# Fused attention and spectral layer: the first q stack on ACT's queue, a load in four, a table and fills in other places

## The chip, the cores and the metric

The kernel runs on one core of one Trainium2 chip. A core has five engines that run their own instruction lists and meet through semaphores: TensorE (PE, matmuls; PEld are its weight loads), VectorE (DVE), ScalarE (ACT), GpSimd (POOL) and SyncE (SP), which here only issues DMAs. SP, ACT and POOL can each issue DMAs; the transfers run on 16 DMA engines. The metric is the device time of one execution in microseconds (us); lower is better.

## The reference

One layer of a transformer with two branches over the same normalized input `xn`. With x of 2 x 2048 x 256 float32:

```python
xn = _layernorm(x, axis=-1)
x = x + _L0_attn_ref(xn, wq, wk, wv, wo) + _L0_ffn_ref(xn, w_freq_real, w_freq_imag, bias)

# attention: 16 q heads of 16, 4 k/v heads shared by groups of 4, rotary, causal
q = _apply_rope((x @ wq).reshape(Bx, Sx, 16, 16), cos, sin)
k = _apply_rope((x @ wk).reshape(Bx, Sx, 4, 16), cos, sin)
v = (x @ wv).reshape(Bx, Sx, 4, 16)
scores = where(causal, einsum('bshd,bthd->bhst', q, k) / 4, -inf)      # k, v broadcast to 16 heads
out = einsum('bhst,bthd->bshd', softmax(scores), v).reshape(Bx, Sx, 256) @ wo

# "ffn": a product in the frequency domain
y = real(ifft(fft(x) @ (w_freq_real + 1j * w_freq_imag))) + bias
```

The second branch is linear in `xn`, so the kernel forms one 256 x 256 matrix of it once (`mff`) and multiplies by that.

## The kernel before, in words

**Blocks and units.** The 4096 rows are cut into eight blocks n of 512 rows (`blocks`, two batches b by four positions j, b running fastest). A block has four units g, each of four q heads: 32 units. For each block: load x (`load_x`, L166), row statistics (`row_stats`, L233, on DVE), the power -1/2 (`row_power`, L241, on POOL), the shift -mean/std (`row_shift`, L247, on DVE), normalization (`norm`, L398, on DVE for block 0, on POOL for the others), PE transposes (`transpose_x`, L405), three projections with `features` (L419): c = 2 gives k and v, c = 0 and 1 the q of two units each. `other_half` (L438) makes a copy with the rotary halves swapped, for blocks 0 and 1 by a PE product and for the rest by DMA; `rotate` (L514) applies cos and sin from a table that `rotary_table` (L276) makes for each j (DVE expands it, PE turns it); `split` (L531) cuts the float32 result into three bf16 parts h, m and l.

**Stacks.** The score products run in bf16 over stacked parts: for each unit a tile `qst` holds seven 16-row groups of q parts, for each block a tile `kst` the matching seven of k. `stack` (L483) fills them by seven 64 KB DMAs straight from the parts (k of every block, and q of unit 0 of block 0); `stack_runs` (L495) takes all other q through DRAM with four larger ones. All of these are issued by SP, through `later` (L389), in one list per block (`sends`).

**Scores.** For each unit the kernel first makes the scores with rows in partitions, to take the row maxima (`maxima`, tiles `sm`, DVE reduces them at L636), writes the negative maxima as three more rows of the q stack (`spread`, with an ACT copy and an ACT-issued DMA of 12 KB), then makes the scores with keys in partitions (`scores`, tiles `st`), ACT takes the exponential (L745), and PE multiplies with v and a column of ones (`values`, tiles `av`, L780). Sums and values go through DRAM to be divided (`put`, `gather`, `invert`, `widen`, `scale`), and `output` (L895) adds both branches to x.

**Order.** The program order of every engine is written by a planner at build time (from L922): each step carries modelled costs and a list of what it needs (`use`, `send`, `through_bank`), steps wait in `streams`, and a loop picks the next PE step: scores ("B"), maxima ("A"), values ("V"), or filling work ("F" and "M": transposes, projections, spectral products). The planner's modelled clocks only choose the order; on the chip engines wait for real semaphores. Three PSUM banks of the ring "st" serve scores, projections and all fillers. Each SP, ACT or POOL instruction list runs strictly in its order.

**The start.** PE first runs 48 transposes of a unit matrix that nothing uses (L968), as a warm-up. `ones` (L370) fills the constant columns of v and rows of k, on DVE for block 0 and on POOL for the others. After the statistics of block 0, `load_late` (L217) has POOL issue six loads of weights. The spectral matrix is made in six PE pieces (tiles `ps_ff` and `ps_mff`) that serve as filling work before and between the first maxima. In the order before, DVE takes block 0's shift, then expands the table of j = 0, then normalizes block 0; DVE takes block 2's statistics just before the first maxima; POOL normalizes block 1 together with block 2, from 34.78 us on, so that block 1's projections come after the first maxima.

Of the kernel before, what the change touches and what calls it, by code (L numbers as in the profile page):

```python
# [23 lines left out]
def tile_attn_plus_spectral_ffn(  # L24
# [29 lines left out]
    nc = tc.nc  # L54
# [96 lines left out]
    def product(to, lhsT, rhs, start, stop):  # L151


        for q in range(0, P, QD):
            nc.tensor.matmul(  # L155
                to[q : q + QD], lhsT[:, q : q + QD], rhs, start=start, stop=stop
            )


    def block_rows(n):  # L160
        b, j = blocks[n]
        return x[b, j * SB : (j + 1) * SB, :].rearrange("(i p) d -> p i d", p=P)
# [1 line left out]
    xt = {}  # L164

    def load_x(n):  # L166
        send("sp", 512, [slot("xt")], [("xt", "in", n)])
        take_slot("xt")
        xt[n] = work.tile([P, NI, D], F32, tag="xt", bufs=2, name=f"xt{n}")
        nc.sync.dma_start(out=xt[n], in_=block_rows(n))  # L170

    take_slot("qst"), take_slot("qst")
    load_x(0)
# [43 lines left out]
    def load_late():  # L217

        for name, src, tag, bufs in (
            ("wre", w_re, "inv", 2), ("dc", dft[0], "inv", 2),  # L220
            ("wim", w_im, "attT", 2), ("ds", dft[1], "avs", 3),
        ):
            take_slot(tag)
            spec[name] = work.tile([P, NK, D], F32, tag=tag, bufs=bufs, name=name)
            nc.gpsimd.dma_start(out=spec[name], in_=src.rearrange("(c p) n -> p c n", p=P))
            send("pool", 256, (), ["spec"])
        nc.gpsimd.dma_start(out=wo_sb, in_=wo.rearrange("(c p) n -> p c n", p=P))
        nc.gpsimd.dma_start(out=bias_sb, in_=bias.partition_broadcast(P))
# [4 lines left out]
    def row_stats(n, i):  # L233
        if i == 0:
            mv[n] = work.tile([P, NI, 2], F32, tag="mv", bufs=2, name=f"mv{n}")
        st = work.tile([P, 6], F32, tag="bn", bufs=3, name=f"bn{n}_{i}")
        nc.vector.bn_stats(st, xt[n][:, i, :])
        nc.vector.bn_aggr(mv[n][:, i, :], st)
        use("dve", 0.53, [("xt", "in", n)], [("mv", n)])

    def row_power(n):  # L241
        rstd[n] = work.tile([P, NI], F32, tag="rs", bufs=2, name=f"rs{n}")
# [3 lines left out]

    def row_shift(n):  # L247
        shift[n] = work.tile([P, NI], F32, tag="sh", bufs=2, name=f"sh{n}")
        nc.vector.scalar_tensor_tensor(
            shift[n], mv[n][:, :, 0], -1.0, rstd[n], ALU.mult, ALU.mult  # L250
        )
        use("dve", 0.2, [("rs", n)], [("sh", n)])

# [125 lines left out]
    def project(n):  # L379
# [2 lines left out]
        b, j = blocks[n]  # L382
        e, eng = (nc.vector, "dve") if n == 0 else (nc.gpsimd, "pool")
        MULT, SUB, CAST, NORM = (0.72, 0.72, 0.46, 0.33) if n == 0 else (1.23, 1.13, 0.63, 0.53)
        raw, sw, swp, part, ra, at = {}, {}, {}, {}, {}, {}
        sends = []
        streams.append(sends)

        def later(out, in_, kb, needs, gives):  # L389


            def go():
                nc.sync.dma_start(out=out, in_=in_)
                send("sp", kb, needs, gives)

            sends.append((-1, -1, "sp", needs, [], go))

        def norm(i):  # L398
            e.tensor_scalar(
                xt[n][:, i, :], xt[n][:, i, :], rstd[n][:, i : i + 1], shift[n][:, i : i + 1],  # L400
                ALU.mult, ALU.add,
            )
            use(eng, NORM, [("sh", n)], [("xn", n, i)])

# [11 lines left out]
            if c == NK - 1:  # L416
                there["xt", n] = clock["pe"]

        def features(c):  # L419
            ps = bank(f"ps_q{n}_{c}")  # L420
            for k in range(NK):
                product(
                    ps, wp[:, k, c, :], xnT[n][:, k, :], start=(k == 0), stop=(k == NK - 1)
                )
            raw[c] = work.tile([P, SB], F32, tag="raw", bufs=3, name=f"raw{n}_{c}")
            at[c] = take_slot("raw")
            nc.scalar.copy(raw[c], ps)  # L427
            through_bank(
                1.83, ["wp", *(("xnT", n, k) for k in range(NK))], "act", 0.48, [("raw", "in", n, c)],
                [("raw", at[c] - ring["raw"])],  # L430
            )
            if n >= 2:
                other_half(c)
# [49 lines left out]
        def stack(c, a_part, f):  # L483
            src = part[c][f * HP : (f + 1) * HP, "hml".index(a_part), :]
            for a in range(len(QPART)):
                if (KPART if c == NK else QPART)[a] == a_part:
                    to = kst[n] if c == NK else qst[n, 2 * c + f]
                    gives = []
                    if a == len(QPART) - 1 if c == NK else a_part == "l":
                        gives = [("kst", n) if c == NK else ("stk", n, 2 * c + f)]  # L490
                        gives += [("part", at[c, "part"])] * (c == NK)
                    needs = [("part", "in", n, c, a_part)]
                    later(to[a * DH : (a + 1) * DH, :, :], src, 64, needs, gives)

        def stack_runs(c, units):  # L495

# [71 lines left out]
        ]  # L568
        for c in (NK, 0, 1):
            table = [("cs", j, 1)] * (n >= 2)  # L570
            pe.append(("pe", ["wp", *table, *xs], ["st", "raw"] + ["sw"] * (n >= 2), lambda c=c: features(c)))
            if n < 2:
                pe.append(("pe", [("raw", "in", n, c)], ["st", "sw"], lambda c=c: other_half(c)))
            if c == NK:
                pe.append(("pe", [("raw", "in", n, NK), ("ones", n)], ["st"], proj_v))
# [383 lines left out]
    def stream(pieces, since=-1, by=-1):  # L959
        streams.append([(since, by, *p) for p in pieces])  # L960
        return streams[-1]
# [11 lines left out]
        row_stats(0, i)  # L973
    row_power(0)
    load_late()
    row_shift(0)
    order_weights()

    def chain(n, starts, late=0):

        norms, pe, rot = project(n)
        eng = norms[0][0]
        stats = [("dve", [("xt", "in", n)], [], lambda i=i: row_stats(n, i)) for i in range(NI)]
        stats.append(("pool", [("mv", n)], [], lambda: row_power(n)))
        stats.append(("dve", [("rs", n)], [], lambda: row_shift(n)))
        s = starts
        if n > 1:
            stream([("sp", [], ["xt"], lambda: load_x(n))], s["load"], s["load"])
        if n:
            stream([("pool", [], [], lambda: ones(n))], s["ones"], s["stats"])  # L990
            stream(stats, s["stats"], s["stats"] + late + 1)
        out_pe = streams.append([]) or streams[-1]
        for k, p in enumerate(pe):
            at = s["pe"] + (k // 2 if n > 1 else 0)
            out_pe.append((at, at + late + 1, *p))
        out_rot = streams.append([]) or streams[-1]
        for p in norms:
            out_rot.append((s["stats"], s["stats"] + late + 2, *p))
        for c, more in ((K, 0), (Q0, 2), (Q1, 5)):
            at = s["rot"] + (more if n > 1 else 0)  # L1000
            for k, p in enumerate(rot[c]):
                out_rot.append((at, at + late + 2 + k // 2, *p))

    def table(j, since):
        expand, turn = rotary_table(j)
        last = [("cs used", at_block[B - 1, j - 2])] if j >= 2 else []
        stream(
            [("dve", last, ["raw", "raw2"], expand)]
            + [("pe", [("trx", j)], ["st"], lambda a=a: turn(a)) for a in range(2)],
            since, since + 3,  # L1010
        )
# [243 lines left out]
```

## Time and profile before

| what | value |
|---|---|
| median of 3 runs (lowest to highest) | 925.84 us (924.08 to 927.47) |
| profiled execution: own time, span | 926.44 us, 924.70 us |
| PE busy | 904.6 us, 98% |
| DVE busy | 748.0 us, 81% |
| ACT busy | 653.7 us, 71% |
| POOL busy | 370.1 us, 40% |
| mean granted clock of PE | 0.995 of full speed |
| chain that ended last, by engine | PE 89%, DVE 5%, ACT 3%, issue, DMA and POOL 1% each |

The span is the time from the first to the last instruction in the record; the execution's own time is 1.74 us longer. Busy shares are of the span. PE is busy nearly throughout, so an idle microsecond of another engine counts only where PE stands and waits for it; such waits can be read from the list of waits and from PE's timeline, each with the line of the instruction that waited and of the one that released it. "issue" names time in which an engine waited for nothing that the profile shows. The granted clock is the share of full speed at which PE was allowed to run.

### The profile page before, as it was taken

The page shows a single profiled execution, that of the slowest core. Times are in us where ns is not written, and L with a number is a line of the kernel's source. Part 1 is how long each engine was busy: PE and PEld are TensorE (multiplying, and loading weights), DVE is VectorE, ACT ScalarE, POOL GpSimd, SP SyncE. Part 2 cuts the span into 40 slices and gives each one's busy share as a digit, 9 for nine tenths or more (in the row PEclk, how much of TensorE's full clock was granted, in tenths as well). Part 3 has the DMA queues.
Part 4 walks back from the last instruction along what each step waited for, and adds up shares of the span by engine and source line. Part 5 has one row for each costly group of instructions (what it writes and reads, how often), then busy time and mean ns, then how long its engine had stood idle before and what let it go on. Part 6 is the DMA issues. An engine that isn't in the chain of part 4 may idle for free.

```text
span 924.7 us, 38985 instructions
## 1 busy us (share of the span) xinstructions
PE 904.6 (98%) x17324; PEld 500.5 (54%) x17324; DVE 748.0 (81%) x1056; ACT 653.7 (71%) x1375; POOL 370.1 (40%) x556
## 2 busy tenths in 40 slices
PE   7999899999999999999999999999999999999997
PEld 4666565655555555555555555555455554645443
DVE  6878697789789996998995999979789988788601
ACT  3266565587757784888865777857688878588784
POOL 7298666824672424822236520311572021102111
PEclk9999999999999999999999999999999999999999
DMA  5435823341244011440002500010133001100000
GB/s 165 119 90 143 199 92 106 97 132 38 65 121 124 27 38 34 112 129 26 14 27 85 150 28 13 27 60 14 31 109 88 15 3 38 49 14 15 27 1 24
DMA packets 41992, 62.13 MB, mean 67 GB/s; under 512 B 8840, under 2 KB 32120, under 8 KB 41824
## 3 DMA queue, kind: packets, MB, share of 16 engines
q1 hardware_dynamic: 32400, 41.18, 16.5%
q0 software_dynamic: 8128, 17.69, 5.9%
q8 instruction: 135, 2.21, 1.0%
q10 hardware_dynamic: 1296, 0.79, 0.3%
q14 instruction: 33, 0.27, 0.1%
HBM read 32.75 MB, written 18.40 MB: 55 GB/s over the span
## 4 chain that ended last, share of the span: by engine, by line
PE 89%; DVE 5%; ACT 3%; issue 1%; DMA 1%; POOL 1%; ACTq 0%; SPq 0%; DVEq 0%; POOLq 0%
PE av L780 24%; PE st L155 22%; PE sm L155 17%; PE sm L631 7%; PE po L155 6%; PE ps_q L155 4%; DVE mx L636 2%; PE sp L155 2%; PE sm L627 2%; PE st L738 2%; ACT es L745 1%; PE ps_x L411 1%; PE st L734 1%; ACT es L747 1%; PE ps_m L671 0%
## 5 line engine op out<-in xcount | busy, mean ns | idle before, releaser
L636 DVE TENSOR_REDUCE mx<-sm 128x2 f32<-128x1024 f32 (+3 forms) x640 | 648.9, 1057 | 87.4 <-PE sm L631 44.1
L745 ACT ACTIVATE es<-st 128x512 f32<-128x512 f32 (+3 forms) x1194 | 552.4, 543 | 179.2 <-PE st L155 145.6
L155 PE MATMUL st<-qst,kst 115*32 115x512 bf16 (+3 forms) x4264 | 327.2, 354 | 1.1 <-ACT es L745 0.4
L780 PE MATMUL av<-es,va 128*32 128x512 f32 (+3 forms) x2560 | 299.9, 529 | 0.6 <-issue 0.3
L155 PE MATMUL sm<-kst,qst 112*32 112x512 bf16 x3072 | 239.1, 379 | 0.1
L155 PEld LDWEIGHTS <-kst 115*32 115x32 bf16 x4608 | 161.1, 95 | 140.6 <-issue 64.8
L752 POOL TENSOR_SCALAR_AFFINE_SELECT es<-es 128x256 f32<-128x256 f32 x192 | 76.7, 406 | 276.0 <-ACT es L745 234.8
L155 PEld LDWEIGHTS <-qst 112*32 112x32 bf16 x3072 | 96.0, 96 | 93.0 <-issue 64.8
L631 PE MATMUL sm<-kst,qst 112*32 112x32 bf16 (+15 forms) x2048 | 122.3, 281 | 0.3 <-issue 0.3
L627 PE MATMUL sm<-mask,ident_h 128*32 128x128 bf16 (+3 forms) x2048 | 100.2, 201 | 1.8 <-DVE mx L636 1.0
L780 PEld LDWEIGHTS av<-es,va 128*32 128x32 f32 x2560 | 85.1, 109 | 28.6 <-ACT avs L791 2.6
L631 PEld LDWEIGHTS <-qst 112*32 112x32 bf16 x2048 | 66.3, 97 | 34.3 <-issue 20.6
L627 PEld LDWEIGHTS <-ident_h 128*32 128x32 bf16 x2048 | 66.1, 96 | 32.2 <-issue 25.5
L906 DVE TENSOR_TENSOR xr<-po,xr 128x256 f32<-128x256 f32 x36 | 15.2, 424 | 51.5 <-PE po L155 49.5
L803 POOL DMA_DIRECT2D res<-avs x30 | 18.2, 606 | 82.7 <-ACT avs L791 79.9
L155 PE MATMUL ps_q<-xnT,wp 128*32 128x512 f32 x384 | 45.4, 600 | 0.0
L747 ACT ACTIVATE es<-sp 128x1024 f32<-128x1024 f32 (+3 forms) x43 | 36.6, 907 | 7.6 <-PE sp L155 7.4
L427 ACT COPY raw<-ps_q 128x512 f32<-128x512 f32 x24 | 14.1, 585 | 35.0 <-PE ps_q L155 35.0
L518 POOL TENSOR_TENSOR ra<-raw,cs 128x512 f32<-128x512 f32 (+1 forms) x21 | 27.4, 1304 | 24.2 <-ACT raw L427 23.0
L738 PE MATMUL st<-qst,kst 115*32 115x480 bf16 (+15 forms) x512 | 36.8, 284 | 0.1
L155 PE MATMUL po<-wo_sb,attT 128*32 128x256 f32 x512 | 34.4, 379 | 0.7 <-ACT attT L869 0.7
L155 PE MATMUL po<-mff,xnT 128*32 128x256 f32 x512 | 34.4, 380 | 0.0
(108 smaller groups left out, 657.0 us busy)
## 6 DMA issues: line engine op xcount, KB each, us to landing
qst<-run SPq DMA_DIRECT2D x62, 128.0 KB
res<-avs POOLq DMA_DIRECT2D x30, 256.0 KB, 3.0
run<-part SPq DMA_DIRECT2D x31, 192.0 KB
qst<-run SPq DMA_DIRECT2D x31, 192.0 KB
xt<-in_L_attn_x_dram SPq DMA_DIRECT2D x8, 512.0 KB
xr<-in_L_attn_x_dram SPq DMA_DIRECT2D x16, 256.0 KB
out_dram<-xr SPq DMA_DIRECT2D x16, 256.0 KB
sw<-raw SPq DMA_DIRECT2D x60, 64.0 KB
```

Of the source, the lines that this page charges most:

```text
L155: nc.tensor.matmul(to[q : q + QD], lhsT[:, q : q + QD], rhs, start=start, stop=stop)
L518: e.tensor_tensor(ra[c][:r], raw[c][:r], cs[j][:r, 0, :], ALU.mult)
L627: nc.tensor.matmul(to[:, at:wd], ident_h[:, q : q + QD], mask[:, q:], start=True, stop=True, skip_group_check=True,)
L631: nc.tensor.matmul(to[:, : at + QD], rows[:, q : q + QD], keys[:, : at + QD], start=False, stop=True, skip_group_check=True,)
L636: nc.vector.tensor_reduce(t["mx"][:, i, 2 * pr : 2 * pr + 2, k], ps[0][:, :, :wd], AX.X, ALU.max)
L738: nc.tensor.matmul(to[:, at:], keys[:, q : q + QD], rows[:, at:], start=False, stop=True, skip_group_check=True,)
L745: nc.scalar.activation(es[u, t, pr][:, e, lo:], ps[:, lo:], AF.Exp, scale=SCALE)
L747: nc.scalar.activation(es[u, t, pr][:, :, lo:], wide[pr][:, :, lo:], AF.Exp, scale=SCALE)
L752: nc.gpsimd.affine_select(out=es[u, t, pr][:, :, lo : lo + P], in_=es[u, t, pr][:, :, lo : lo + P], pattern=[[0, 2], [1, P]], compare_op=A ...
L780: nc.tensor.matmul(av[u][QD * h : QD * (h + 1), lo:], va[at_block[b, t // NI]][:, t % NI, h, :], es[u, t, h // 2][:, h % 2, lo:], start=(t ...
L803: nc.gpsimd.dma_start(out=res[n, c][f], in_=avs[u])
L906: nc.vector.tensor_tensor(xr[n, r][:, e, :], po, xr[n, r][:, e, :], ALU.add)
```

## The change

It has these parts:

- Block 0's x is loaded by four DMAs of 128 KB in place of one of 512 KB, and each statistics step needs only its own quarter.
- The expansion of the first rotary table (`table_0[0]()`) stands ahead of block 0's shift on DVE.
- The shift becomes mean/std, subtracted by `norm`; for blocks 1 to 7 it moves from DVE to POOL.
- The seven DMAs that stack unit 0 of block 0 are issued by ACT (`line=2`), with a list of their own; block 0's k stack and its q runs get separate SP lists.
- `features` is cut into two PE steps, one for each half of the contraction, between which the planner may place others.
- In the planner, the fills of blocks 1 to 7 and their powers need block 0's last k part (`first_keys`), and block 2's statistics need the finished maxima of unit 0 of block 0 (`rows_0`).

In the built program this gives a new order in the first 60 us: block 1 is normalized right after its power, on POOL; its transposes, its k/v and its first q projection stand before the first maxima on PE, and half of the spectral pieces after them; ACT's list has, after the two copies of block 1's transposes, four stack issues, then the copy of raw, an issue, a copy of a spectral piece, an issue, the copy of sw, an issue. Block 2's statistics stand after the first maxima of unit 0, its normalization in the middle of block 1's rotation on POOL. SP sends six of block 1's seven k stack DMAs before the q stacks of units 2 and 3 of block 0. Later the order on all engines differs in small ways.

```diff
     def load_x(n):
-        send("sp", 512, [slot("xt")], [("xt", "in", n)])
+        at = slot("xt")
         take_slot("xt")
         xt[n] = work.tile([P, NI, D], F32, tag="xt", bufs=2, name=f"xt{n}")
-        nc.sync.dma_start(out=xt[n], in_=block_rows(n))
+        step = NI if n else 1
+        for i in range(0, NI, step):
+            send("sp", 128 * step, [at], [("xt", "in", n, k) for k in range(i, i + step)])
+            nc.sync.dma_start(out=xt[n][:, i : i + step, :], in_=block_rows(n)[:, i : i + step, :])
...
     def row_shift(n):
         shift[n] = work.tile([P, NI], F32, tag="sh", bufs=2, name=f"sh{n}")
-        nc.vector.scalar_tensor_tensor(
-            shift[n], mv[n][:, :, 0], -1.0, rstd[n], ALU.mult, ALU.mult
-        )
-        use("dve", 0.2, [("rs", n)], [("sh", n)])
+        e, eng, us = (nc.vector, "dve", 0.2) if n == 0 else (nc.gpsimd, "pool", 0.25)
+        e.tensor_tensor(shift[n], mv[n][:, :, 0], rstd[n], ALU.mult)
+        use(eng, us, [("rs", n)], [("sh", n)])
...
-        sends = []
-        streams.append(sends)
-
-        def later(out, in_, kb, needs, gives):
-
+        lines = [[], [], []]
+        streams.extend(lines)
+
+        def later(out, in_, kb, needs, gives, line=0):
+
+
+            eng = "act" if line == 2 else "sp"
 
             def go():
-                nc.sync.dma_start(out=out, in_=in_)
-                send("sp", kb, needs, gives)
-
-            sends.append((-1, -1, "sp", needs, [], go))
+                (nc.scalar if line == 2 else nc.sync).dma_start(out=out, in_=in_)
+                send(eng, kb, needs, gives)
+
+            lines[line].append((-1, -1, eng, needs, [], go))
...
-                ALU.mult, ALU.add,
+                ALU.mult, ALU.subtract,
...
-        def features(c):
-            ps = bank(f"ps_q{n}_{c}")
-            for k in range(NK):
-                product(
-                    ps, wp[:, k, c, :], xnT[n][:, k, :], start=(k == 0), stop=(k == NK - 1)
-                )
+        def features(c, k):
+            if k == 0:
+                held[c] = bank(f"ps_q{n}_{c}"), take_slot("st")
+            ps, at_st = held[c]
+            product(ps, wp[:, k, c, :], xnT[n][:, k, :], start=(k == 0), stop=(k == NK - 1))
+            use("pe", 0.9, ["wp", ("xnT", n, k), ("st", at_st - ring["st"])], [("ps", at_st)])
+            if k < NK - 1:
+                return
...
-                    later(to[a * DH : (a + 1) * DH, :, :], src, 64, needs, gives)
+                    later(
+                        to[a * DH : (a + 1) * DH, :, :], src, 64, needs, gives,
+                        2 if c < NK else 1 if n == 0 else 0,
+                    )
...
-            pe.append(("pe", ["wp", *table, *xs], ["st", "raw"] + ["sw"] * (n >= 2), lambda c=c: features(c)))
+            pe.append(("pe", ["wp", *table, xs[0]], ["st", "raw"] + ["sw"] * (n >= 2), lambda c=c: features(c, 0)))
+            pe.append(("pe", [xs[1]], [], lambda c=c: features(c, 1)))
...
     load_late()
+    table_0 = rotary_table(0)
+    table_0[0]()
     row_shift(0)
...
-        stats = [("dve", [("xt", "in", n)], [], lambda i=i: row_stats(n, i)) for i in range(NI)]
-        stats.append(("pool", [("mv", n)], [], lambda: row_power(n)))
-        stats.append(("dve", [("rs", n)], [], lambda: row_shift(n)))
+        first_keys = [("part", "in", 0, NK, "l")]
+        rows_0 = [("np", 0, 0)] * (n == 2)
+        stats = [("dve", [("xt", "in", n, i), *rows_0], [], lambda i=i: row_stats(n, i)) for i in range(NI)]
+        stats.append(("pool", [("mv", n), *first_keys], [], lambda: row_power(n)))
+        stats.append(("pool", [("rs", n)], [], lambda: row_shift(n)))
...
-            stream([("pool", [], [], lambda: ones(n))], s["ones"], s["stats"])
+            stream([("pool", first_keys, [], lambda: ones(n))], s["ones"], s["stats"])
```

More of the change, by code (lines that the diff above doesn't have):

```diff
@@ L238, in row_stats @@
         nc.vector.bn_aggr(mv[n][:, i, :], st)
-        use("dve", 0.53, [("xt", "in", n)], [("mv", n)])
+        use("dve", 0.53, [("xt", "in", n, i)], [("mv", n)])
     def row_power(n):
@@ L384, in project @@
         MULT, SUB, CAST, NORM = (0.72, 0.72, 0.46, 0.33) if n == 0 else (1.23, 1.13, 0.63, 0.53)
-        raw, sw, swp, part, ra, at = {}, {}, {}, {}, {}, {}
-        sends = []
-        streams.append(sends)
-        def later(out, in_, kb, needs, gives):
+        raw, sw, swp, part, ra, at, held = {}, {}, {}, {}, {}, {}, {}
+        lines = [[], [], []]
+        streams.extend(lines)
+        def later(out, in_, kb, needs, gives, line=0):
+            eng = "act" if line == 2 else "sp"
             def go():
-                nc.sync.dma_start(out=out, in_=in_)
-                send("sp", kb, needs, gives)
-            sends.append((-1, -1, "sp", needs, [], go))
+                (nc.scalar if line == 2 else nc.sync).dma_start(out=out, in_=in_)
+                send(eng, kb, needs, gives)
+            lines[line].append((-1, -1, eng, needs, [], go))
         def norm(i):
@@ L427, in features @@
             nc.scalar.copy(raw[c], ps)
-            through_bank(
-                1.83, ["wp", *(("xnT", n, k) for k in range(NK))], "act", 0.48, [("raw", "in", n, c)],
-                [("raw", at[c] - ring["raw"])],
+            use(
+                "act", 0.48, [("ps", at_st), ("raw", at[c] - ring["raw"])],
+                [("st", at_st), ("raw", "in", n, c)],
             )
@@ L1004, in table @@
     def table(j, since):
-        expand, turn = rotary_table(j)
+        expand, turn = rotary_table(j) if j else table_0
         last = [("cs used", at_block[B - 1, j - 2])] if j >= 2 else []
         stream(
-            [("dve", last, ["raw", "raw2"], expand)]
+            [("dve", last, ["raw", "raw2"], expand)] * (j > 0)
             + [("pe", [("trx", j)], ["st"], lambda a=a: turn(a)) for a in range(2)],
```

## The prediction

> **What bounds the kernel now.** I read the page first, then busy time by stretch, then TensorE's (PE's) waits, then the chain and the timelines of the first 55 us.
>
> ```profile
> PE 904.6 (98%) x17324; PEld 500.5 (54%) x17324; DVE 748.0 (81%) x1056; ACT 653.7 (71%) x1375; POOL 370.1 (40%) x556
> PEclk9999999999999999999999999999999999999999
> ```
>
> PE is busy 904.6 of 924.7 us at almost full clock. No edit changes the number of columns that PE multiplies, so only what PE loses can be won: 20.1 us of idling, and time at a lowered clock. Where it lies (us from the start; stretch, its length, then busy time by engine):
>
> ```profile
> 0.00:25.00 25.00, 20.25 (x157) 12.21 (x161) 17.55 (x49) 8.12 (x16) 16.41 (x36) 0.93 0.52 161
> 25.00:50.00 25.00, 24.44 (x527) 15.35 (x523) 19.86 (x42) 7.85 (x17) 9.79 (x14) 1.00 0.38 103
> ...
> 100.00:125.00 25.00, 21.29 (x655) 15.63 (x655) 18.71 (x33) 16.06 (x44) 15.75 (x24) 0.93 0.61 163
> ```
>
> 4.75 us are idle in the first 25 us, where 7.14 us more are 48 warm-up transposes that compute nothing; 3.7 us in 100 to 125. The end (875 to 925) idles 8.0 us, and no edit touches it. In the two early stretches the third last number, the granted clock, is 0.93. PE's waits name the causes:
>
> ```profile
> PE st L734 <- issue: 2.2, 1, 2.2
> PE ps_tr L305 <- DVE trx L293: 1.8, 1, 1.8
> ...
> PE ps_x L411 <- POOL xt L399: 0.2, 1, 0.2
> ```
>
> The second is the start. Its chain (start, length, what):
>
> ```profile
> 0.80 4.43 DMA xt<-in_L_attn_x_dram
> ...
> 7.90 1.06 POOL rs L244
> 8.96 0.02 issue
> 8.98 0.16 DVE sh L249
> 9.14 1.17 DVE trx L293 x6
> 10.31 0.04 issue
> 10.36 1.11 PE ps_tr L305 x8
> 11.47 0.10 issue
> 11.56 2.32 PE ps_x L411 x8
> 13.88 2.54 PE ps_q L155 x16
> ```
>
> Load, row statistics, the power on POOL, shift, then the rotary table on VectorE (DVE), and only then normalization: the table stands in line although it needs nothing of the statistics. The two PE groups at the end are slow, and the clock by single microseconds says why (third last number):
>
> ```profile
> 9.00:10.00 1.00, 0.00 (x0) 0.00 (x0) 1.00 (x6) 0.53 (x2) 1.00 (x2) 1.00 0.00 0
> 12.00:13.00 1.00, 1.00 (x4) 0.65 (x5) 0.97 (x5) 0.13 (x1) 1.00 (x3) 0.50 0.99 340
> ```
>
> **The start, edit by edit.** *Load in four.* The first statistics began at 5.25, when the 512 KB had landed; DVE's fills end at 4.63. Four 128 KB pieces are issued one per 0.44 to 0.48 us (the length of SP's load issues), in the same order of bytes, so the first two should be there by 4.63 and the last by about 5.2, and statistics start 0.6 earlier. By the waits in the built program SP and ACT share eight completion lanes; block 1's load is now the ninth issue and waits for wk, which landed at 4.97. Block 1 needs it after 10.5: free.
>
> *Table before the shift.* Eight reductions, 1.63 in all, move into POOL's power (7.57 to 8.95). Statistics end at 6.9 instead of 7.47, table 8.5, power 8.35, shift 8.7 instead of 9.14, and the four normalizations (1.89) follow at once instead of at 10.61: 1.9 earlier. The table's input must have landed by 6.9; it is queued behind the first load only, at 192 KB beside 512 KB in some 3 us. At worst it lands with the last bytes, 7.6, and 0.7 of the 1.9 goes.
>
> *The clock.* The warm-up ends at 8.55, the table's transposes now start there, and the 1.80 us hole closes. The Trainium skill, "TensorE: Matmul & The Clock Gate" (section "HAM oscillation — how this bites in real kernels"), asks for no idle gap over about 3.4 us; by it this hole cost 1.8 and nothing more. The trace differs: after it the clock is 0.50 from 11.7 to 15.1, and again from 107.3 to 110.7 after a hole of 2.2; two gaps of 0.7 us each (16.4, 20.4) did nothing. The measurement decides: 3.4 us at half speed cost 1.7. Block 0's transposes then take 1.25 instead of 2.32. Walked through: transposes from 9.65 to 11.4 (last normalized piece 10.6), copies to 12.05, first projection done at 13.2 instead of 16.42. **3.2 us early**, of which DVE's parts and PE's third projection (20.5 instead of 23.7) inherit all; by the skill's rule it would be 1.5.
>
> *Block 1's projection as the next filling.* It replaces half of the spectral products as PE's work ahead of the first scores, and needs POOL's normalization of block 1: power done at 8.35, six load issues (4.46), two fills of 2.55, power 1.6, shift 0.3, four normalizations at 0.54 end at 21.95. PE arrives at 20.5 and would take 0.62: **1.0 lost**.
>
> *First q stack by ACT.* SP had all fourteen stack issues in one line:
>
> ```profile
> 20.10 4.50 SPq L393 DMA_DIRECT2D kst<-part  x7
> 24.73 5.03 SPq L393 DMA_DIRECT2D qst<-part  x7
> ```
>
> so the stack landed at 32.0 although its last part was made at 26.6. On ACT the seven have their own line, but ACT runs in order: four issues come after both copies of block 1's transposes (23.4), then copy raw, issue, copy of a spectral product, issue, copy sw, and the last. With 0.65 to 0.72 per issue the last ends near 29.6 and lands 2.2 later (as SP's last, 29.76 to 32.0), at 31.8. PE gets there at 31.9, with 2.2 us more of work behind it; its old waits of 0.33 (31.7) and 0.21 (38.06) go: **0.5 won**. What queues behind ACT's issues is POOL's rotation of block 1, which needs sw (29.0). SP also sends block 1's keys before the q units 2 and 3, which land near 43; units 2 starts after 49: free.
>
> *Block 2 behind the first maxima.* Its normalization now follows most of block 1's rotation on POOL. From 29.0: k 6.53 (as 46.93 to 53.46), q0 7.83, half of q1 3.98, power 1.4, cast 0.7, shift 0.3, subtraction 1.24, normalization 2.15: 53.1. PE, from 31.9 by its own rows, comes to block 2's transposes near 51.5. The wait is 0 if POOL's start is 1.5 earlier and 2.5 if PE meets no other wait; the near row (0.21 for the same wait) pulls down, the sum says 1.3. I take **1.0 lost**.
>
> *The rest.* Shift on POOL for the other blocks: DVE stood 1.04 in it at 228.16, and PE then idled 0.62 for DVE: **0.6 won**. Projections in two pieces: the same eight products, which already waited for each half separately (begun at 13.81, second half copied at 14.5); they only let scores stand between. Fills "behind" block 0's parts keep their place on POOL, after the loads, and nothing waits: nothing. The sign in the normalization: nothing.
>
> **The hole at 104.7.** PE stopped at 104.68 in the middle of a tile, for no semaphore. The instruction queue's packets (16 KB each) began at 93.38, 98.06 and 104.44; the DMA share was 1.02 in 102 to 104. So a fetch came late. "Runtime: NRT & Kernel Launch" (section "Instruction fetch mechanics") calls fetching mostly hidden; by it the change gains nothing here. The trace prices the hole at 2.19 and 1.7 of half clock. The same transfers follow in the same order, but PE and they shift by microseconds. Bounds: nothing (it recurs), 3.9 (gone). The half clock needs nearly the whole length, so a hole cut by half costs 1.1; I take **1.0 won**, near the recurring end, since the burst stays.
>
> **Sum.** 3.2 - 1.0 + 0.5 - 1.0 + 0.6 + 1.0 = 3.3. The profiled execution took 926.44 (span 924.70), so 923.1; it lies 0.6 over the median of the runs, 925.84, from which I get **922.5**.
>
> **Rivals.** *Hole gone, the rest as summed*: 2.9 more, 919.6. For it: it takes a fetch delayed by nearly 5 us. Against: DMA is at 0.95 or more in four of the two-us stretches from 98 to 114.
>
> *Gain given back at block 2's transposes*: the wait is the full 2.5, and such a hole starts another half clock: 1.5 + 1.7 lost, 925.7, no change. Speaks for it: POOL has no gap from 29 on. Against: PE's row waits on POOL are 0.2 in all.
>
> *Slower: ACT's queue blocks.* Its fifth and seventh stack issue wait for the landing of the first and third (same lanes). At 2.2 a landing that is free; in the full DMA stretches a POOL gather needs 4.2, and at that each would wait about 2. Copy of sw, and so POOL's chain, come 4 later: PE waits 5 instead of 1, and 1.7 of half clock: 4 + 1.7 = 5.7, 928.2. It ends above 925.84 once the two waits exceed 1.7 together. Against: around 25 us the DMA share is low.
>
> *The hole recurs in full, twice*: 1.0 + 3.9, 927.4.
>
> **How the numbers follow.** Forecast 0.40 (919.5 to 925), hole gone 0.20, given back 0.25, ACT's queue or a second hole 0.15. About 0.3% (2.8 us, below 923.1 or above 928.6) is what a measurement can tell here. Faster: 0.6 of the first, nearly all of the second, a tenth of the third: 0.45 + 0.03, with little from elsewhere, 0.50. Slower: half of the last and a little of the third, 0.12. Range for 8 in 10: 917.5 to 927.8.
>
> **What would show it.** Right: normalization near 8.7, no half clock before 20 us, first projection's end near 13.2, first scores near 32 after block 1's first two projections. Wrong: statistics still after 5.2 or the table after 7.6 (load step); a PE wait on POOL's xt over 2 us near 51 (block 2 step); ACT issues with gaps between (queue step); an "issue" wait of 2 us elsewhere (hole).

## The result, and the profile after

The changed kernel is slower: 936.59 us median (934.77 to 940.40, 6 runs) against 926.83 (924.08 to 927.66, 6 runs) of the kernel before, run beside it. The ratio is 1.0114, 95% interval 1.0091 to 1.0138. I had forecast 922.5 and a range up to 927.8. The profiled execution took 937.86 us, its span 936.1; that of before 926.44 and 924.7. The span is 11.4 us longer.

First the page of the changed kernel, the rows of busy time and of the granted clock:

```profile
PE 908.8 (97%) x17324; PEld 500.8 (54%) x17324; DVE 749.0 (80%) x1049; ACT 655.0 (70%) x1375; POOL 391.9 (42%) x563
PEclk9899999999999999999999999999999999999999
```

PE has the same 17324 matmuls, yet 4.2 us more of busy time, and it idles 27.3 us in place of 20.1 (span less busy). POOL is 21.8 us busier, with seven instructions more. Stretches of the changed kernel, read as before: length, busy time by engine, then the granted clock as the third last number:

```profile
0.00:25.00 25.00, 18.54 (x134) 11.76 (x134) 20.05 (x52) 7.94 (x16) 19.06 (x35) 0.97 0.54 163
25.00:50.00 25.00, 24.15 (x425) 13.31 (x429) 13.88 (x29) 7.05 (x14) 18.93 (x22) 0.89 0.48 118
50.00:75.00 25.00, 21.81 (x592) 15.17 (x584) 17.79 (x43) 13.66 (x33) 15.95 (x20) 0.93 0.52 131
100.00:125.00 25.00, 20.74 (x625) 15.32 (x623) 17.69 (x38) 14.99 (x39) 17.72 (x23) 0.93 0.71 181
```

The first 75 us are worse: PE was busy 20.25, 24.44 and 24.95 there before, with the clock down in the first row only. The third of these rows of the kernel before is

```profile
50.00:75.00 25.00, 24.95 (x651) 14.55 (x649) 18.98 (x49) 16.50 (x39) 22.80 (x26) 1.00 0.44 112
```

The stretch of 100 to 125 is as poor as it was. PE's waits point to the cause at once:

```profile
PE ps_x L415 <- POOL xt L403: 9.2, 10, 1.4
PE av L790 <- issue: 3.2, 2, 2.7
...
PE st L748 <- issue: 1.1, 1, 1.1
```

The first wait was 0.2 us, once. PE's transposes of x now stand behind POOL's normalization ten times. Why that is late is in the durations of that line, here in the changed kernel (ns: least, median, most):

```profile
L403 POOL TENSOR_SCALAR xt<-xt,rs,sh x28: 1208/1212/1767, 20.5 to 661.4; 128x256 f32<-128x256 f32 x28
...
L403 DVE TENSOR_SCALAR xt<-xt,rs,sh x4: 396/446/550, 8.6 to 9.6; 128x256 f32<-128x256 f32 x4
```

and in the kernel before:

```profile
L399 POOL TENSOR_SCALAR xt<-xt,rs,sh x28: 545/548/561, 34.8 to 650.7; 128x256 f32<-128x256 f32 x28
...
L399 DVE TENSOR_SCALAR xt<-xt,rs,sh x4: 396/438/854, 10.6 to 12.1; 128x256 f32<-128x256 f32 x4
```

The same shape, type and operands, but on POOL 1212 ns in place of 548; on DVE nothing happened. The one difference is the second operation, subtract in place of add. 28 times 0.664 is 18.6 us, most of POOL's 21.8. The chain of the changed kernel shows the price at block 1 (start, length, what):

```profile
11.46 1.97 PE ps_q L155 x16
...
18.61 1.46 POOL rs L247
...
20.46 5.81 POOL xt L403 x4
26.27 0.04 issue
26.32 1.33 PE ps_x L415 x5
27.65 1.86 PE ps_sw L155 x8
```

Block 0's first projection does end at 13.43, near the forecast's 13.2; the start came as written. But block 1's four normalizations take 5.81 us where the forecast had 2.16, PE stands in its transposes meanwhile, and then:

```profile
24.00:25.00 1.00, 0.17 (x1) 0.00 (x0) 0.86 (x1) 0.00 (x0) 1.00 (x1) 0.50 0.00 0
```

the clock is at half, from 23.6 to 30.5, and again from 61.2 to 64.6 after block 2's transposes, which waited for the same line. The swap products at 27.65 take 1.86 us in place of 1.1.

### The profile page after: what moved, and what is told of

Same layout as the page of the kernel before. It is cut to its first block, busy times and chain, and to the rows that moved or that the text cites. A ratio compares the mean times of both kernels' runs of the same rounds, so it can differ in the third digit from the quotient of the medians.

```text
span 936.1 us, 39017 instructions
## 1 busy us (share of the span) xinstructions
PE 908.8 (97%) x17324; PEld 500.8 (54%) x17324; DVE 749.0 (80%) x1049; ACT 655.0 (70%) x1375; POOL 391.9 (42%) x563
## 4 chain that ended last, share of the span: by engine, by line
PE 86%; POOL 4%; ACT 4%; issue 2%; DVE 1%; DMA 1%; ACTq 0%; SPq 0%; POOLq 0%
PE av L790 23%; PE st L155 21%; PE sm L155 16%; PE sm L641 6%; PE po L155 6%; PE ps_q L155 4%; POOL xt L403 3%; ACT es L755 2%; PE sm L637 2%; PE sp L155 1%; PE st L748 1%; DVE mx L646 1%; ACT es L757 1%; PE idle L978 1%; PE ps_x L415 1%
## 5 line engine op out<-in xcount | busy, mean ns | idle before, releaser
L155 PE MATMUL st<-qst,kst 115*32 115x512 bf16 (+3 forms) x4264 | 331.0, 354 | 1.0 <-ACT es L755 0.2
L155 PEld LDWEIGHTS <-kst 115*32 115x32 bf16 x4608 | 158.8, 95 | 152.8 <-issue 77.9
L641 PE MATMUL sm<-kst,qst 112*32 112x64 bf16 (+15 forms) x2048 | 123.0, 282 | 0.0
L155 PE MATMUL ps_q<-xnT,wp 128*32 128x512 f32 x384 | 48.8, 601 | 0.3 <-ACT xnT L418 0.3
L748 PE MATMUL st<-qst,kst 115*32 115x192 bf16 (+15 forms) x512 | 37.7, 286 | 1.1 <-issue 1.1
L527 POOL TENSOR_TENSOR ra<-raw,cs 128x512 f32<-128x512 f32 (+1 forms) x21 | 26.9, 1279 | 23.6 <-ACT raw L433 22.7
L403 POOL TENSOR_SCALAR xt<-xt,rs,sh 128x256 f32<-128x256 f32 x28 | 34.8, 1249 | 0.6
```

The costliest lines, as they stand in the source:

```text
L155: nc.tensor.matmul(to[q : q + QD], lhsT[:, q : q + QD], rhs, start=start, stop=stop)
L403: e.tensor_scalar(xt[n][:, i, :], xt[n][:, i, :], rstd[n][:, i : i + 1], shift[n][:, i : i + 1], ALU.mult, ALU.subtract,)
L527: e.tensor_tensor(ra[c][:r], raw[c][:r], cs[j][:r, 0, :], ALU.mult)
L641: nc.tensor.matmul(to[:, : at + QD], rows[:, q : q + QD], keys[:, : at + QD], start=False, stop=True, skip_group_check=True,)
L748: nc.tensor.matmul(to[:, at:], keys[:, q : q + QD], rows[:, at:], start=False, stop=True, skip_group_check=True,)
```

## The experiments

**Theory A:** the multiply-and-subtract form is slow on POOL, and its late results make the loss through PE's waits and the half clock that they start. **Rival B:** the new order makes it: ACT's line of issues, the moved fills, block 2 behind the first maxima. The medians of the runs, each with the kernel before of the same chip:

| kernel | us | before | ratio (95%) |
|---|---|---|---|
| changed, add (e1_add) | 925.47 | 925.28 | 0.9997 (0.9982 to 1.0011) |
| before, subtract (e2_before_sub) | 939.37 | 925.28 | 1.0143 (1.0086 to 1.0199) |
| changed, subtract then multiply (e3_sub_mult) | 935.91 | 925.28 | 1.0090 (1.0056 to 1.0123) |
| changed, subtract in blocks 3 to 7 only (e4_sub_late) | 929.36, one run | 925.78 | |
| before, new start alone (e5_start) | 923.98 | 925.78 | 0.9977 (0.9965 to 0.9989) |
| add, q stack on SP (e6_stack_sp) | 929.28 | 925.78 | 1.0031 (1.0011 to 1.0052) |
| add, fills late (e7_fills_late) | 923.55 | 925.78 | 0.9968 (0.9954 to 0.9981) |
| add then multiply (e8_add_mult) | 927.72, one run | 925.99 | |
| e7 with the q stack on SP (e9_sp_same_order) | 923.76 | 925.99 | 0.9978 (0.9967 to 0.9990) |
| subtract, fills late (e10_sub_fills_late) | 931.40 | 925.99 | 1.0060 (1.0039 to 1.0081) |

**The changed kernel with add.**

```diff
...
-        e.tensor_tensor(shift[n], mv[n][:, :, 0], rstd[n], ALU.mult)
...
+        if n == 0:
+            nc.vector.scalar_tensor_tensor(shift[n], mv[n][:, :, 0], -1.0, rstd[n], ALU.mult, ALU.mult)
+        else:
+            nc.gpsimd.tensor_tensor(shift[n], mv[n][:, :, 0], rstd[n], ALU.mult)
+            nc.gpsimd.tensor_scalar(shift[n], shift[n], -1.0, None, ALU.mult)
...
-                ALU.mult, ALU.subtract,
+                ALU.mult, ALU.add,
```

> The changed kernel with the normalization as multiply and add again; the negative shift of blocks 1 to 7 is made on POOL by one more small instruction, everything else in the same order on every engine. Theory A (the pair of operations is slow on POOL): a normalization of 128x256 is back at 0.55 us, block 1's four end about 3.4 us earlier, PE's waits on POOL's xt fall from 9.2 us to under 2, the half-clock stretches from 23.6 to 30.5 and at 61 go, and the time falls to 922 to 927. Rival B (the new order and the queue of ACT are the cause): the pair may become faster, but the time stays at 933 or more, since ACT's stack issues and block 2's late normalization remain.

It took 925.47, 11.1 us less than the changed kernel (10.8 by their ratios to the kernel before, since the two were not run side by side). Its durations on that line, and PE's wait for it:

```profile
L403 POOL TENSOR_SCALAR xt<-xt,rs,sh x28: 548/552/1095, 20.9 to 648.4; 128x256 f32<-128x256 f32 x28
...
PE ps_x L415 <- POOL xt L403: 2.2, 5, 0.6
```

The duration is back, the waits fall from 9.2 to 2.2 us (a little above my "under 2"), and its profile has no half clock before the end. B asked for 933 or more with this order: it falls as the cause of the loss. The two profiled executions, 937.86 and 924.18, differ by 13.7. PE idles 6.2 us more in the first: 7.0 more of waits on POOL, a little less elsewhere. It is busy 7.4 us more, and 6.8 of that is the changed kernel's three half-clock stretches before the end (6.8 us once and 3.4 twice, 13.6 us in all), which cost half their length. The last of them, at 115.8, follows an "issue" wait of 2.73 and is not POOL's.

**The kernel before with subtract.**

```diff
-        nc.vector.scalar_tensor_tensor(
-            shift[n], mv[n][:, :, 0], -1.0, rstd[n], ALU.mult, ALU.mult
...
+        nc.vector.tensor_tensor(
+            shift[n], mv[n][:, :, 0], rstd[n], ALU.mult
...
-                ALU.mult, ALU.add,
+                ALU.mult, ALU.subtract,
```

> The kernel before with only the sign moved: shift is the product of mean and power, and the normalization multiplies and subtracts; every instruction keeps its place. Theory A: POOL's normalization takes 1.21 instead of 0.55 us each, the eight that stand together at 34.8 end at 44.5 instead of 39.1, PE waits there 2 to 5 us on POOL's xt and perhaps gets one more half-clock stretch (1.7): 929 to 933. Theory B: the operation is as fast as before, or slow without harm: within 1 us of the kernel before, 926 to 928.

The moved sign alone costs the kernel before some 13 to 14 us (interval 8 to 18). The direction is A's, the size is not: I had counted only the eight normalizations at 34.8. They take 9.65 us,

```profile
34.71 9.65 POOL L399 TENSOR_SCALAR xt<-xt,rs,sh 128x256 f32<-128x256 f32 x8
...
38.40 0.33 PE L411 MATMUL ps_x<-ident,xt 128*128 128x128 f32 x1 [0.96 <-POOL xt L399]
39.60 0.33 PE L411 MATMUL ps_x<-ident,xt 128*128 128x128 f32 x1 [0.87 <-POOL xt L399]
40.80 0.33 PE L411 MATMUL ps_x<-ident,xt 128*128 128x128 f32 x1 [0.87 <-POOL xt L399]
42.01 0.33 PE L411 MATMUL ps_x<-ident,xt 128*128 128x128 f32 x1 [0.88 <-POOL xt L399]
```

and PE waits 3.6 there, with a half clock after it, from 42.4 to 45.8. But its waits on this line come to 8.0 in all, 11 of them: the later blocks have little slack too.

**Which form is slow.**

```diff
-                xt[n][:, i, :], xt[n][:, i, :], rstd[n][:, i : i + 1], shift[n][:, i : i + 1],
-                ALU.mult, ALU.subtract,
+                xt[n][:, i, :], xt[n][:, i, :], mv[n][:, i, 0:1], rstd[n][:, i : i + 1],
+                ALU.subtract, ALU.mult,
```

> The changed kernel with the normalization written as (x - mean) * power, that is subtract first and multiply second, straight from the statistics; the shift is still made but not used. It asks which pair is slow on POOL. If only a subtraction in second place is slow: 0.55 us each and 922 to 927. If every pair but multiply-and-add is slow: 1.21 us each and 935 to 938, as the changed kernel. Theory B says nothing of the duration and expects 933 or more in either case.

The second answer: 1.21 us each and 935.9. That could mean that only multiply-and-add is fast. So add in first place was tried, from the version with add, with minus the mean in `shift` (the product is still made, and overwritten):

```diff
-            nc.vector.scalar_tensor_tensor(shift[n], mv[n][:, :, 0], -1.0, rstd[n], ALU.mult, ALU.mult)
+            nc.vector.tensor_scalar(shift[n], mv[n][:, :, 0], -1.0, None, ALU.mult)
...
-            nc.gpsimd.tensor_scalar(shift[n], shift[n], -1.0, None, ALU.mult)
+            nc.gpsimd.tensor_scalar(shift[n], mv[n][:, :, 0], -1.0, None, ALU.mult)
...
-                xt[n][:, i, :], xt[n][:, i, :], rstd[n][:, i : i + 1], shift[n][:, i : i + 1],
-                ALU.mult, ALU.add,
+                xt[n][:, i, :], xt[n][:, i, :], shift[n][:, i : i + 1], rstd[n][:, i : i + 1],
+                ALU.add, ALU.mult,
```

> The version with add everywhere, with the normalization as (x + (-mean)) * power, add first and multiply second. It asks whether the subtraction or the pair is slow on POOL. If a subtraction alone is slow: 0.55 us each, about 925. If every pair but multiply-then-add is slow: 1.21 us each, about 936.

The line of the subtract-then-multiply kernel, then that of add-then-multiply:

```profile
L403 POOL TENSOR_SCALAR xt<-xt,mv,rs x28: 1208/1210/1722, 20.3 to 659.8; 128x256 f32<-128x256 f32 x28
```

```profile
L403 POOL TENSOR_SCALAR xt<-xt,sh,rs x28: 553/562/981, 20.8 to 650.6; 128x256 f32<-128x256 f32 x28
```

Of the four forms tried, the two with a subtraction take 1.21 us and the two with an addition 0.55, in either place. "Only multiply-and-add is fast" falls. The one run of add-then-multiply, 927.72, is 2.3 above the median of the version with add and within its runs (922.75 to 928.43); its profile has two half-clock stretches of 3.4 us that the other's has not.

**Where the loss lies.** Blocks 1 and 2 with add, blocks 3 to 7 with subtract, from the version with add:

```diff
-            nc.gpsimd.tensor_scalar(shift[n], shift[n], -1.0, None, ALU.mult)
+            if n < 3: nc.gpsimd.tensor_scalar(shift[n], shift[n], -1.0, None, ALU.mult)
...
-                ALU.mult, ALU.add,
+                ALU.mult, ALU.add if n < 3 else ALU.subtract,
```

> The changed kernel with multiply and add for blocks 1 and 2 and multiply and subtract kept for blocks 3 to 7; order as in the changed kernel. It asks where the slow pair costs its 11 us. Theory A: at the beginning, where PE stands right behind POOL: waits of 5 us and half-clock stretches at 23.6 to 30.5 and 61 to 64.6 (5 us) belong to blocks 1 and 2, so most of the loss goes here: 926 to 929, about 2 us over the version with add everywhere. Rival: the 13 us of extra POOL work in blocks 3 to 7 matter as much, by waits of PE at 233, 450 and 650: 931 or more.

929.36 in one run, 3.9 us over the version with add (I had said 2). Its waits:

```profile
PE ps_x L415 <- POOL xt L403: 5.2, 8, 1.1
PE av L790 <- issue: 3.0, 2, 2.5
```

One run does not fix the share, since runs of one kernel lie up to 5.7 us apart, and this one holds a half clock at 107.8 (1.7 us lost) that follows the "issue" wait of 2.46. The waits fix it better: 5.2 us on the line, in place of 2.2 with add and 9.2 with subtract. The later blocks' waits are 0.5 to 1.1 us each, without a half clock; the larger part, with two half-clock stretches on top (5.1 us lost), belongs to the first two blocks.

**The slow form with the first place out of PE's way.** From the changed kernel:

```diff
-            stream([("pool", first_keys, [], lambda: ones(n))], s["ones"], s["stats"])
+            stream([("pool", [*first_keys, ("xn", 1, NI - 1)], [], lambda: ones(n))], s["ones"], s["stats"])
```

> The changed kernel, multiply and subtract, with only the fills of blocks 1 and 2 moved behind block 1's normalization. It asks whether the slow pair costs by where it stands. Theory A (it costs where PE stands right behind it): block 1's normalization ends near 19.5, ahead of PE at 20.9, so the 4.2 us of waits at 22 to 26 and the half clock from 23.6 go; block 2's waits and those of the later blocks stay: about 7 us less than the changed kernel, 928 to 931. Rival (the added POOL work itself, wherever it is): 934 or more.

931.40 (two runs), 5.2 us less than the changed kernel and 0.4 above A's range, though POOL does the same slow work. So it costs where PE stands behind it, as A says. That it is not the full 7 shows in PE's timeline at block 2:

```profile
53.19 0.33 PE L415 MATMUL ps_x<-ident,xt 128*128 128x128 f32 x1 [1.93 <-POOL xt L403]
54.40 0.33 PE L415 MATMUL ps_x<-ident,xt 128*128 128x128 f32 x1 [0.88 <-POOL xt L403]
55.60 0.48 PE L415 MATMUL ps_x<-ident,xt 128*128 128x128 f32 x1 [0.88 <-POOL xt L403]
56.80 0.48 PE L415 MATMUL ps_x<-ident,xt 128*128 128x128 f32 x1 [0.73 <-POOL xt L403]
```

PE arrives earlier and meets more of the next stall: 4.4 us here against 2.6 in the changed kernel, and a half clock from 55.4 to 62.2 in place of 61.2 to 64.6.

**The start alone**, put into the kernel before: the hunks of `load_x`, `row_stats`, `table_0` and `table`, without the shift and the sign.

```diff
...
+        for i in range(0, NI, step):
...
+            nc.sync.dma_start(out=xt[n][:, i : i + step, :], in_=block_rows(n)[:, i : i + step, :])
...
     load_late()
+    table_0 = rotary_table(0)
+    table_0[0]()
     row_shift(0)
```

> The kernel before with the start alone changed: first load in four pieces, statistics by piece, the rotary table before the shift; every other instruction in its place. By the prediction's steps 1 to 3 block 0's projections end 3.2 us earlier and the half clock after 11.7 goes; nothing else is asked of the start, so by those steps 922 to 923.5. Rival: what is won is given back before the first scores, because the q stack comes by SP's line of fourteen issues and the transposes of block 1 wait for POOL's normalizations of 34.8: 925 to 926, with PE waits of 1 to 2 us at 30 to 40.

The ratio 0.9977 (0.9965 to 0.9989) is a gain of 2.1 us, 1.0 to 3.2; the median lies 0.5 us above the first forecast and 1 us below the rival's. In its profile the clock stays full where it had been half (the first line), and PE waits for the q stack (the second):

```profile
12.00:13.00 1.00, 1.00 (x12) 0.13 (x4) 0.26 (x2) 0.00 (x0) 1.00 (x3) 1.00 0.65 240
...
29.47 0.18 PE L634 MATMUL sm<-kst,qst 112*32 112x32 bf16 x1 [1.02 <-DMA qst<-part]
```

The third projection begins at 18.74. 1.0 us goes back at the q stack (0.33 before), as the rival said; the rest stays. That it stays is read from the medians: this profiled execution is among the slowest of the 20 (926.48) and loses 4.9 us to "issue" waits, where that of before lost 3.4.

**The fills.** The same edit as above, on the version with add: POOL normalizes block 1 ahead of the two fills.

> The version with add everywhere, with POOL's fills of blocks 1 and 2 behind block 1's normalization instead of ahead of it; orders of PE, DVE, ACT and SP are the same. If PE's four waits of together 2.0 us for block 1's normalization at 22 to 24.5 come from the two fills of 2.5 us each in front of it, they go: block 1's normalization ends near 17, before PE's third projection (21.4), and the time falls by 2 us: 923 to 924. Rival: PE then meets the first q stack 2 us earlier and waits there instead (the stack landed at 35.2), so nothing is won: 925 to 926.

The normalization begins at 15.35 in place of 20.88, PE goes from the third projection into the transposes without a wait,

```profile
19.51 1.47 PE L155 MATMUL ps_q<-xnT,wp 128*32 128x512 f32 x12
20.92 1.35 PE L415 MATMUL ps_x<-ident,xt 128*128 128x128 f32 x8
```

and the time is 923.55, 0.9968 of before (0.9954 to 0.9981), against 0.9997 of the version with add. The 2 us are as expected. A wait of 0.65 for the stack appears at 32.2, no worse than the 0.80 it had. This version beats both kernels.

**The q stack on SP.** From the version with add, in two ways; first through the planner, which then moves PE's fillings too:

```diff
-                        2 if c < NK else 1 if n == 0 else 0,
+                        0,
```

> The version with add everywhere, with the seven q stack issues back on SP's one line; the planner then moves some of PE's fillings too. By the prediction's step 5 ACT's line is worth 0.5 us, so this should be 0.5 us slower, with PE's wait on the stack back. Rival: on ACT the issues stand behind block 1's transposes (the last ends at 31.1 and lands at 35.2, where PE waits 0.8), while SP would have issued them by about 28, landed by 30.5: 0.8 us or more faster, no wait on the stack.

929.28, slower, by more than the first view had and against the rival: 0.3% over before. The wait for the first stack is gone, and SP has issued all of it by 26.7. What grew is PE's "issue" waits at 70 to 130, 6.1 us against 4.2 in the version with add, and waits for DVE's maxima (1.4 against 0.5). The planner moved instructions on every engine (115 of ACT's 1375 stand in another order), so this run does not price ACT's line. The second way, from the version with late fills, leaves every other instruction in its place:

```diff
-                (nc.scalar if line == 2 else nc.sync).dma_start(out=out, in_=in_)
+                nc.sync.dma_start(out=out, in_=in_)
```

> The version with fills late, with the seven issues of the first q stack on SP at the places that the plan gave them, so that every other instruction of every engine keeps its place. It measures ACT's line alone. By the prediction's step 5 ACT's line wins 0.5 us, so this is 0.5 us slower (924 to 924.5), with the wait of 0.65 for the stack longer. Rival: on ACT the issues wait behind the copies of block 1, so SP is no later: the wait of 0.65 us at 32.2 goes and the time is 0 to 0.7 us less (923).

The stack wait falls from 0.65 to 0.20 us,

```profile
32.05 0.19 PE L641 MATMUL sm<-kst,qst 112*32 112x32 bf16 x1 [0.20 <-DMA qst<-part]
```

and the time is the same within its error, 923.76 against 923.55 (ratios to before 0.9978 and 0.9968, intervals overlapping). The 0.5 us that ACT's line was to win do not show: with it the wait for the stack is 0.45 us longer, and the times, each uncertain by about 1.2 us, differ by 0.2 (0.9 by the ratios).

## Why the prediction was wrong

**The failed step** is one sentence: "The sign in the normalization: nothing." Behind it stood "four normalizations at 0.54" in the step on block 1 and "normalization 2.15" in that on block 2, both carried over from the rows of multiply-and-add. A changed operation is an operation that the trace does not show, and I had no row for it; it wanted a bound from both sides. With 0.66 more for each, block 1's wait grows from 1.0 to 3.6 us, block 2's as much, and if a half clock follows each (1.7 us lost, as after the 1.80 us hole), the same working would have given 2 x 2.64 + 2 x 1.7 = 8.7 us more, 931.2 (an estimate made with the result in hand), and with it the right direction. The runs set the step's price at some 11 us (13 to 14 in the order before). Of the rivals, "given back at block 2's transposes" had the place and the mechanism for a share of it, but without a cause of that size.

With the sign put back, the other steps can be read in the version with add, for which the sum was 922.5 and which took 925.47 (it has one small POOL instruction more in blocks 1 to 7):

- *Load in four, table before the shift*: right. Statistics at 4.66 (forecast: 0.6 ahead of 5.25) and normalization at 8.60 (8.7) in the changed kernel. In the version with add DVE waited 0.30 us for the table's input, the risk that the forecast named, and normalization began at 8.95.
- *The clock*: right. No half clock before 20 us in any of the kernels with the new start; first projection done at 13.43 (13.2), third at 20.9 (20.5) where it was 23.7. Of "3.2 us early" 2.8 is there in the changed kernel, 2.3 in the version with add; by itself in the kernel before the start gained 2.1 (1.0 to 3.2).
- *Block 1's projection as the next filling*: mechanism right, size off. PE waited 2.0 us (0.63, 0.37, 0.64, 0.37) and not 1.0. POOL began at 20.88 and not near 19.8 (0.35 of it is the added sign instruction), and took 3.46 us for the four where 2.16 was counted.
- *First q stack by ACT*: wrong. 0.80 us of wait in place of 0.33 and 0.21, and a wait 0.45 us shorter when it alone is undone. The last issue ends at 31.1 and not at 29.6, since the issues stand behind the copies of block 1's transposes, and these are late.
- *Block 2 behind the first maxima*: 0.21 us in the version with add and 0.85 with late fills; 1.0 was counted. Right in kind; that it is so small with add is in part because PE comes late itself.
- *Shift on POOL*: 225 to 250 us has PE busy 24.82 where it was 24.38: 0.4 of the 0.6.
- *The hole at 104.7*: the likelier end came, it recurs. The "issue" waits from 70 to 130 us and the half clock behind them cost 3.1 + 1.7 before, 4.5 + 1.7 in the changed kernel, 4.2 with add, 3.5 + 1.7 with late fills. With add that is 0.6 won where 1.0 was taken; the sum moves with the order by as much as the step was worth. Why they differ so was not settled. The traces fit the late fetch of the forecast: in all eight kernels with an "issue" wait of over 1.9 us here, a 16 KB packet of the instruction queue began between 0.9 us before the wait and 0.3 us after its start, and such packets come only about every 4 us. No run delayed or hastened a fetch, so this stays argued.

Put together for the version with add: 3.3, less 0.9 of the start, 1.0 of block 1, 0.8 of the stack, 0.4 of the hole and 0.2 of the shift, plus 0.8 of block 2, leaves 0.8 us. The medians say 0 within 1.4, the profiled execution 2.3 (924.18 against 926.44), so the steps at their measured size agree with the medians within that error. The fills ahead of block 1's normalization are what the forecast priced too low: behind it, 2 to 3 us come back.

## What to carry to other kernels

A sign moved from one operand to the operation is a change of instruction: time the new form on the engine that runs it, and bound it from both sides if no row shows it. A slow instruction on an engine that is 40% busy can cost most of its added length, and here a stretch at half clock on top, where the bottleneck engine stands right behind it; moving it ahead of work that nobody waits for (here two fills of 2.5 us) removes the wait, but then the next place where the same instruction stands in front has to be looked at. A plan that issues the same work in another order can make some 3 us of waits elsewhere, so one part is measured best with every other instruction held in its place.

## What the runs showed of the hardware

*Subtraction on POOL.* A 128 x 256 float32 tensor_scalar with two operations and per-row operands takes 0.55 to 0.56 us with multiply and add in either order, and 1.21 us with a subtraction in either place (medians of 28). On DVE it makes no difference (0.44 with add in the kernel before, 0.45 with subtract in the changed one).

*The half clock needs no gap of 3.4 us, and what starts it stays open.* The Trainium skill, "TensorE: Matmul & The Clock Gate" (section "HAM oscillation — how this bites in real kernels"), gives a rule of no idle gap over about 3.4 us. Here single waits of 1.80 and 2.19 us were followed by 3.4 us at half, others of 1.92 (start-alone kernel) and 2.05 us (q stack on SP) by none. Four waits of 1.40, 1.08, 0.95 and 0.72 within 5.4 us were followed by 6.8 us at half. Four of 0.63, 0.37, 0.64 and 0.37 within 3 us were followed by none with add, while four of nearly the same length at the same place in the add-then-multiply run were followed by 3.4 us. In the last kernel with the q stack on SP (e9) still less was enough; PE's four waits for block 2, then the clock from 56 to 57:

```profile
52.07 0.33 PE L415 MATMUL ps_x<-ident,xt 128*128 128x128 f32 x1 [0.71 <-POOL xt L403]
52.61 0.33 PE L415 MATMUL ps_x<-ident,xt 128*128 128x128 f32 x1 [0.22 <-POOL xt L403]
53.15 0.33 PE L415 MATMUL ps_x<-ident,xt 128*128 128x128 f32 x1 [0.21 <-POOL xt L403]
53.69 0.33 PE L415 MATMUL ps_x<-ident,xt 128*128 128x128 f32 x1 [0.21 <-POOL xt L403]
...
56.00:57.00 1.00, 1.00 (x26) 0.72 (x20) 1.00 (x2) 0.20 (x1) 1.00 (x3) 0.50 0.34 72
```

These waits are 1.35 us in sum, and the clock was at half from 55.1 to 58.5. So neither the longest wait nor the sum tells which waits are followed by a half clock, and the forecast's "The half clock needs nearly the whole length" does not hold in general. The stretches are about 3.4 us or twice that. The measurement decides: no gap of 3.4 us is needed.

*POOL beside DVE.* Block 1's four normalizations took 3.46 us, block 2's 2.18, in the same kernel. In the first, DVE ran the rotation of block 0. Timelines of DVE and POOL in the version with add:

```profile
21.02 0.69 DVE L535 TENSOR_TENSOR raw<-ra,sw 128x512 f32<-128x512 f32 x1
...
22.29 0.92 DVE L557 TENSOR_TENSOR rb<-raw,part 128x512 f32<-128x512 f32 x1
```

```profile
20.88 3.46 POOL L403 TENSOR_SCALAR xt<-xt,rs,sh 128x256 f32<-128x256 f32 x4
...
53.06 2.18 POOL L403 TENSOR_SCALAR xt<-xt,rs,sh 128x256 f32<-128x256 f32 x4
```

The Trainium skill, "SBUF — State Buffer" (section "Who interferes with whom"), says that a DVE instruction with two SBUF inputs contends with a GpSimd instruction that reads SBUF. The trace agrees in that the four are 1.28 us slower beside such instructions and casts. The changed kernel has the same in its single normalizations of block 1, first and last of the four:

```profile
20.46 1.77 POOL L403 TENSOR_SCALAR xt<-xt,rs,sh 128x256 f32<-128x256 f32 x1
...
25.05 1.21 POOL L403 TENSOR_SCALAR xt<-xt,rs,sh 128x256 f32<-128x256 f32 x1
```

The first three (1.77, 1.41 and 1.44 us) ran beside DVE's rotation; during the last DVE did nothing, and it took the usual 1.21. But with late fills one that ran 0.41 us beside such a product took 0.56 all the same, and no run was made to take DVE's work away, so this cause is argued and not shown.
